# The last four sequences' stages of a four-layer stack get issue times of their own

## The chip, the cores and the metric

The kernel runs on one core of one Trainium2 chip. The metric is the device time of one execution in microseconds (us), the median of several runs. The core has engines with a queue each: PE (matrix multiply, with its weight loads), DVE (vector), ACT (scalar functions), POOL (general) and SP, which here only issues transfers. Each serves its queue in the order in which the program puts it.

## The reference

Sixteen sequences of 512 tokens with 256 features pass through four layers, each with a normalization before it and a residual sum behind it:

```
x = x + mamba(layernorm(x))        # a state scan over the 512 tokens, 16 states
x = x + fp4_ffn(layernorm(x))      # gate, up, down; 704 hidden
x = x + linear_attention(layernorm(x))   # 16 heads, causal
x = x + fp4_ffn(layernorm(x))      # the same weights again
```

An `fp4_linear` rounds its input in blocks of 16 to the nearest of eight magnitudes times a block scale, and multiplies with weights rounded likewise. The sequences are independent of each other. Within a sequence the four layers follow each other.

## The kernel before

**Stages.** All matrix products are in float32. For each sequence `b` there are four stages, written as Python generators that yield a number, their own estimate of the work just recorded:

- `scan(b)` (L850): `mamba` of `b` woven with `prologue` of `b + 1` (norm, projections, and the step sizes `dt` written to DRAM as `dd`). `mamba` takes 16 steps. In each, `spread` loads a decay tile `bar` by DMA from `dd` (four buffers, issued three steps ahead), ACT takes two exponentials and a square of it (L527, L530), DVE runs the scan (L548) and a multiply (L552) into `h`, and PE sums over the states into `py` (L558). After each half, `py` is copied to `yT` (L565), transposed (`pt_y`, L568) and added to `x` (L571).
- `ffn(0, "f", b)`: layer norm on DVE (L392 to L405, the power on POOL, L394), the rounding `fp4` (L230 to L252: `amax`, `half`, `inv`, `v`, `big`, with ACT's `big` at L248 in the middle), transposes `pt_f` (L418), then four chunks of 128 tokens. For each chunk `hidden` makes `pg` and `pu` (L605), the gated product `h` (L611 to L613) and its rounding, and `down` transposes it (`pt_h`, L627), copies it on ACT (`hqT`, L631 and L636), multiplies (`po`, L640) and adds to `x` (L377).
- `attention(b)`: `rstd` of the statistics, `pt_a` (L426, which waits for `diag_a`, made on ACT at L424 from `rstd`), `pqk` (L678), the feature maps (L684 to L686), the running key sums `run` and `pden` (L816 to L823), and then per chunk `pv`, `psc` (L722), the masked scores `sm` (L729), `pn` (L753), its copy `num` on ACT (L760), `pr` (L768), `yT` (L773), the state update `pkv` and `kv`, and the projection `pro` (L800) with its sum into `x` (L377).
- `last_ffn(b)`: the same FFN code under the letter `g`; its sum into `x` is L647, and then `x` goes out by DMA.

A tile's name carries the stage's letter; in this text its sequence is told in words ("`po_g` of 14, chunk 3").

**The order.** `run_all` (L865) decides in which order the stages' instructions are recorded. Each stage has a begin, a length and a total (`SCAN`, `FFN`, `ATTN`); it keeps a clock that starts at its begin and moves on by the yielded number times length over total, and the stage with the earliest clock records its next piece. The unit is one sequence: scan `b` begins at `b`, its first FFN at `b + 1`, its attention at `b + 2.1` and its last FFN at `b + 3.1`. So in the steady part four sequences are under way, each in another stage. After recording, the framework's scheduler places the instructions in each engine's queue, by readiness and by the recorded order as priority; the recorded order therefore shifts the queues but is not copied into them.

Behind sequence 15 there is no further scan, so the kernel drains: its first FFN is recorded beside attention 14 and the last FFN of 13, its attention beside the last FFN of 14, and its last FFN alone.

Of the kernel before, what the change touches and what calls it, by code (L numbers as in the profile page):

```python
# [32 lines left out]
def kernel(  # L33
# [19 lines left out]
    B, S, D = x.shape  # L53
# [37 lines left out]
    def load(b):  # L91
        xt = xp.tile([P, NC, D], F32, tag="x", name=f"x_{b}")
        nc.sync.dma_start(xt, x[b].rearrange("(c p) d -> p c d", p=P))
        return xt

    xs = [load(0)]
# [766 lines left out]
    SCAN, FFN, ATTN = 65.7, 40.2, 25.7  # L863

    def run_all(stages):  # L865


        under_way = []
        while stages or under_way:
            if not under_way or (stages and stages[0][0] <= min(u[0] for u in under_way)):  # L870
                begin, length, total, stage, *args = stages.pop(0)
                under_way.append([begin, length / total, stage(*args)])
                continue
            now = min(under_way, key=lambda u: u[0])
            try:
                now[0] += next(now[2]) * now[1]
            except StopIteration:
                under_way.remove(now)
# [12 lines left out]

    stages = []
    for b in range(B):
        if b > 0:
            stages.append((b, 1.0, SCAN, scan, b))
        stages.append((b + 1.0, 1.0, FFN, ffn, 0, "f", b, xs))
        stages.append((b + 2.1, 0.9, ATTN, attention, b, xs))
        stages.append((b + 3.1, 0.6, FFN, last_ffn, b))
    run_all(sorted(stages, key=lambda stage: stage[0]))


# [27 lines left out]
```

## Time and profile before

| | |
|---|---|
| Median of 3 runs | 2825.38 us (2824.58 to 2828.75) |
| The profiled execution | 2823.49 us, its span 2821.8 us |
| Mean granted clock of PE | 0.942 |
| PE busy | 2449.7 us, 87% of the span |
| DVE busy | 2430.5 us, 86% |
| ACT busy | 1492.1 us, 53% |
| The chain that ended last | DVE 40%, PE 36%, DMA 9%, ACT 9%, issue 3% |
| Loads of `bar` | 256 of 511 KB, 4.7 us each from issue to landing |

All times inside the execution are counted from the span's start. A float32 product shows as two PE records, a transpose as one. The busy time of an engine is the union of its records; PE's records are pipelined, so a busy PE is not PE at its peak. The granted clock is the share of full speed that PE's clock was given in a stretch. In a line of a timeline the columns are start, duration, engine, source line, operation, tiles written and read, shape, count, and in brackets the idle time before it with what ended it. In a line of the waits they are who waited for whom, the total in us, how often, and the longest.

### The profile page before, as it was taken

To read this page: it belongs to the slowest core of one execution; us is meant where nothing else is said; L and a number is where in the kernel's file an instruction comes from. 1 tells how busy PE (TensorE), PEld (TensorE's weight loads), DVE (VectorE), ACT (ScalarE), POOL (GpSimd) and SP (SyncE) were. 2 spreads that over 40 slices of the span, in tenths; PEclk is the share of its full clock that TensorE was granted. 3 is DMA by queue.
4 is the path that set the end of the run, shared out by engine and by line. 5 is a ranking of instruction groups with operands and counts; after the bars stand their busy time and mean duration, and the time that the engine had idled before them with its cause. 6 is when DMAs were issued, how large, how long until landed. Compare 5 with 4: busy or idle time off the path is not lost.

```text
span 2821.8 us, 34272 instructions
## 1 busy us (share of the span) xinstructions
PE 2449.7 (87%) x12907; PEld 1441.9 (51%) x12907; DVE 2430.5 (86%) x3689; ACT 1492.1 (53%) x2846; POOL 172.2 (6%) x171
## 2 busy tenths in 40 slices
PE   5677989799898989989898998989899898889886
PEld 3234545455555555555555555555555554556564
DVE  7898888898999898899989889998988999868465
ACT  4776564465646455464645556464555646333321
POOL 2000000000000010000001000000100000000000
PEclk7788999899999999999999999999999999999897
DMA  5533212222223131322313132131213213000000
GB/s 142 131 93 82 64 49 53 67 53 83 52 60 76 38 75 45 82 53 54 82 38 75 45 82 53 47 89 38 75 45 83 53 45 82 24 8 1 8 8 8
DMA packets 97146, 165.01 MB, mean 58 GB/s; under 512 B 8434, under 2 KB 92372, under 8 KB 96980
## 3 DMA queue, kind: packets, MB, share of 16 engines
q1 hardware_dynamic: 95360, 161.77, 22.3%
q8 instruction: 101, 1.65, 0.3%
q10 hardware_dynamic: 1620, 1.06, 0.1%
q14 instruction: 65, 0.53, 0.1%
HBM read 146.02 MB, written 16.78 MB: 58 GB/s over the span
## 4 chain that ended last, share of the span: by engine, by line
DVE 40%; PE 36%; DMA 9%; ACT 9%; issue 3%; POOL 2%; SPq 0%; POOLq 0%; ACTq 0%; DVEq 0%
DVE h L548 15%; DMA bar<-dd 9%; PE pg_g L605 5%; DVE h L552 4%; PE pu_g L605 4%; PE po_g L640 4%; PE pg_f L605 3%; PE pu_f L605 3%; PE py L558 3%; ACT bar L527 2%; PE pz L457 2%; DVE v_f L244 2%; DVE sm L729 2%; PE pqk L678 2%; ACT bar L530 1%
## 5 line engine op out<-in xcount | busy, mean ns | idle before, releaser
L548 DVE TENSOR_TENSOR_SCAN h<-bar,inp 128x1024 f32<-128x1024 f32 x256 | 579.4, 2277 | 13.9 <-PE py L558 7.6
L527 ACT ACTIVATE bar<-bar,a_col 128x511 f32<-128x511 f32 x512 | 352.4, 715 | 339.6 <-DMA bar<-dd 291.5
L558 PE MATMUL py<-h,red 128*32 128x512 f32 x1024 | 288.7, 645 | 119.3 <-DVE h L552 118.2
L552 DVE TENSOR_TENSOR h<-h,cm 128x1024 f32<-128x1024 f32 x256 | 311.1, 1218 | 0.6
L530 ACT ACTIVATE bar<-bar 128x1022 f32<-128x1022 f32 x256 | 269.3, 1052 | 3.0
L640 PE MATMUL po_g<-wdT,hqT_g 128*128 128x256 f32 (+1 forms) x768 | 214.3, 425 | 41.8 <-ACT hqT_g L631 41.8
L640 PEld LDWEIGHTS po_g<-wdT,hqT_g 128*128 128x128 f32 (+1 forms) x768 | 149.0, 206 | 120.3 <-ACT hqT_g L631 65.1
L640 PE MATMUL po_f<-wdT,hqT_f 128*128 128x256 f32 (+1 forms) x768 | 198.2, 400 | 9.6 <-ACT hqT_f L631 9.6
L605 PE MATMUL pg_g<-wgT,tT_g 128*128 128x352 f32 x512 | 190.7, 492 | 0.3 <-DVE sm L729 0.3
L640 PEld LDWEIGHTS po_f<-wdT,hqT_f 128*128 128x128 f32 (+1 forms) x768 | 137.5, 192 | 94.6 <-ACT hqT_f L636 29.0
L605 PE MATMUL pu_g<-wuT,tT_g 128*128 128x352 f32 x512 | 182.3, 480 | 0.0
L605 PE MATMUL pg_f<-wgT,tT_f 128*128 128x352 f32 x512 | 181.8, 478 | 0.0
L605 PE MATMUL pu_f<-wuT,tT_f 128*128 128x352 f32 x512 | 172.7, 460 | 3.4 <-DVE sm L729 3.0
L729 DVE TENSOR_TENSOR sm<-psc,causal 128x512 f32<-128x512 f32 x256 | 163.9, 681 | 10.8 <-PE psc L722 5.9
L611 ACT ACTIVATE h_g<-pg_g 128x352 f32<-128x352 f32 x128 | 59.1, 462 | 195.3 <-PE pg_g L605 195.1
L558 PEld LDWEIGHTS py<-h,red 128*32 128x32 f32 x1024 | 37.8, 110 | 221.6 <-DVE h L552 171.4
L605 PEld LDWEIGHTS pu_g<-wuT,tT_g 128*128 128x128 f32 x512 | 103.3, 202 | 60.7 <-issue 11.4
L763 POOL COPY dx<-den 128x256 f32<-128x256 f32 x64 | 42.2, 660 | 1482.7 <-PE pr L768 795.5
L248 ACT ACTIVATE big_f<-v_f 128x704 bf16<-128x704 f32 (+1 forms) x80 | 67.2, 840 | 122.3 <-DVE v_f L244 122.3
L605 PEld LDWEIGHTS pg_f<-wgT,tT_f 128*128 128x128 f32 x512 | 96.3, 196 | 66.9 <-issue 23.2
L612 DVE SCALAR_TENSOR_TENSOR h_g<-h_g,pg_g 128x352 f32<-128x352 f32 x128 | 65.5, 512 | 74.2 <-ACT h_g L611 72.8
L678 PE MATMUL pqk<-tT_a,w_qkv_sb 128*128 128x512 f32 x256 | 121.6, 614 | 7.4 <-ACT tT_a L430 7.4
(237 smaller groups left out, 4707.0 us busy)
## 6 DMA issues: line engine op xcount, KB each, us to landing
bar<-dd SPq DMA_DIRECT2D x256, 511.0 KB, 4.7
x<-in_L_attn_a_x_dram SPq DMA_DIRECT2D x16, 512.0 KB, 4.5
dd<-dt SPq DMA_DIRECT2D x128, 64.0 KB, 1.7
out_dram<-x SPq DMA_DIRECT2D x16, 512.0 KB, 4.4
w_qkv_sb<-in_L_attn_b_W_attn_dram ACTq DMA_DIRECT2D x1, 768.0 KB, 7.1
raw_d<-in_L_ffn_w_down_dram SPq DMA_DIRECT2D x1, 704.0 KB
raw_g<-in_L_ffn_w_gate_dram SPq DMA_DIRECT2D x1, 640.0 KB, 7.1
raw_u<-in_L_ffn_w_up_dram SPq DMA_DIRECT2D x1, 640.0 KB, 6.5
```

The source lines that it names most:

```text
L248: nc.scalar.activation(big, v, AF.Abs, scale=STEP)
L527: nc.scalar.activation(bar[:, i, 1:S], bar[:, i, 1:S], AF.Exp, scale=a_col[:, g : g + 1])
L530: nc.scalar.activation(bar[:, :, 1:S], bar[:, :, 1:S], AF.Square)
L548: nc.vector.tensor_tensor_scan(h.rearrange("p i t -> p (i t)"), bar.rearrange("p i t -> p (i t)"), inp.rearrange("p i t -> p (i t)"), 0.0, ...
L552: nc.vector.tensor_tensor(h, h, cm.unsqueeze(1).to_broadcast([P, 2, S]), ALU.mult)
L558: nc.tensor.matmul(py[32 * q : 32 * q + 32, :], red[:, j, :], (h0, h)[q // 2][:, q % 2, :], start=False, stop=(j == 3),)
L605: nc.tensor.matmul(pw[:, :HF], xqT[:, k, ts(c, P)], wT[:, k, cols], start=(k == 0), stop=(k == ND - 1),)
L611: nc.scalar.activation(hc, pg[:, :HF], AF.Tanh, scale=0.5)
L612: nc.vector.scalar_tensor_tensor(hc, hc, 1.0, pg[:, :HF], ALU.add, ALU.mult)
L640: nc.tensor.matmul(po[:, :D], hqT[:rows, r, :], wdT[:rows, r, :], start=(r == 0), stop=(r == NR - 1),)
L678: nc.tensor.matmul(pz, w_qkv_sb[:, k, ts(je, P)], xnT[:, k, :], start=(k == 0), stop=(k == ND - 1),)
L729: nc.vector.tensor_tensor(t, psc[g].rearrange("p (s t) -> p s t", t=P), causal.unsqueeze(1).to_broadcast([P, NH // 4, P]), ALU.mult,)
```

## The change

It gives the last four sequences begins and lengths of their own in `run_all`'s unit. The table is indexed by how far the sequence is from the last one; each entry names a stage (0 scan, 1 first FFN, 2 attention, 3 last FFN), its begin after 15, and its length. The other stages keep the old times, and no stage's code is touched.

```
     stages = []
     for b in range(B):
+        times = [(b, 1.0), (b + 1.0, 1.0), (b + 2.1, 0.9), (b + 3.1, 0.6)]
+
+        for stage, *time in {0: ((0, 0.0, 0.75), (1, 0.78, 0.7), (2, 1.5, 0.5), (3, 2.02, 0.4)), 1: ((1, 0.0, 0.75), (2, 0.8, 0.65), (3, 1.5, 0.5)), 2: ((2, 0.1, 0.7), (3, 0.9, 0.6)), 3: ((3, 0.1, 0.75),)}.get(B - 1 - b, ()):
+            times[stage] = (B - 1 + time[0], time[1])
         if b > 0:
-            stages.append((b, 1.0, SCAN, scan, b))
-        stages.append((b + 1.0, 1.0, FFN, ffn, 0, "f", b, xs))
-        stages.append((b + 2.1, 0.9, ATTN, attention, b, xs))
-        stages.append((b + 3.1, 0.6, FFN, last_ffn, b))
+            stages.append((*times[0], SCAN, scan, b))
+        stages.append((*times[1], FFN, ffn, 0, "f", b, xs))
+        stages.append((*times[2], ATTN, attention, b, xs))
+        stages.append((*times[3], FFN, last_ffn, b))
     run_all(sorted(stages, key=lambda stage: stage[0]))
```

In begin and end (begin plus length):

| Sequence | Stage | Before | After |
|---|---|---|---|
| 12 | last FFN | 15.1 to 15.7 | 15.1 to 15.85 |
| 13 | attention | 15.1 to 16.0 | 15.1 to 15.8 |
| 13 | last FFN | 16.1 to 16.7 | 15.9 to 16.5 |
| 14 | first FFN | 15.0 to 16.0 | 15.0 to 15.75 |
| 14 | attention | 16.1 to 17.0 | 15.8 to 16.45 |
| 14 | last FFN | 17.1 to 17.7 | 16.5 to 17.0 |
| 15 | scan | 15.0 to 16.0 | 15.0 to 15.75 |
| 15 | first FFN | 16.0 to 17.0 | 15.78 to 16.48 |
| 15 | attention | 17.1 to 18.0 | 16.5 to 17.0 |
| 15 | last FFN | 18.1 to 18.7 | 17.02 to 17.42 |

## The prediction

> **What bounds the kernel now.** I read the page's slices first, then the busy time by stretch of the closing part, then the waits there, then PE's timeline around the longest of them. The two programs as built differ only from 2382.1 us on (PE's first moved instruction; DVE's is at 2390.4, ACT's at 2369.5), so 2382 of the 2821.8 us are the same in both, and I price the rest.
>
> ```profile
> PE   5677989799898989989898998989899898889886
> DVE  7898888898999898899989889998988999868465
> PEclk7788999899999999999999999999999999999897
> ```
>
> One slice is 70.5 us. DVE runs at nine tenths until the last scan ends and then falls to 8, 6, 8, 4, 6, 5; PE stays at 8 or 9 up to the last slice. The drain is bound by PE and by the chain of the last sequence, not by DVE.
>
> ```profile
> core 0: us, PE busy (x) PEld busy (x) DVE busy (x) ACT busy (x) POOL busy (x), PEclk, DMA share, GB/s
> 2382.00:2543.00 161.00, 139.79 (x745) 85.37 (x744) 129.57 (x209) 63.92 (x135) 5.93 (x7) 0.93 0.09 23
> 2543.00:2661.00 118.00, 105.44 (x651) 71.54 (x649) 79.52 (x149) 34.67 (x89) 5.02 (x6) 0.97 0.02 5
> 2661.00:2766.00 105.00, 84.57 (x538) 56.38 (x538) 62.16 (x104) 28.51 (x65) 2.61 (x5) 0.86 0.02 6
> 2766.00:2821.80 55.80, 42.91 (x144) 28.41 (x144) 29.32 (x49) 11.45 (x26) 0.00 (x0) 0.84 0.03 10
> ```
>
> These are four stages, cut where PE starts sequence 15's first FFN (2543), its attention (2661) and its second FFN (2766). I call them A, B, C, D. PE is idle 21, 13, 20 and 13 us in them, 67 in all. Its work is the same in both kernels, so 67 us less what cannot be filled is all that reordering can win, apart from the clock.
>
> ```profile
> DVE x L377 <- PE po_f L640: 15.6, 5, 3.9
> PE pt_g L418 <- DVE xn_g L252: 12.3, 2, 12.1
> PE pt_h_g L627 <- DVE h_g L252: 10.5, 3, 3.9
> PE pt_a L426 <- ACT diag_a L424: 8.9, 2, 5.1
> ACT bar L527 <- DMA bar<-dd: 7.9, 7, 3.0
> ```
>
> Totals, counts, and the longest, from 2382 on. PE's long waits are handovers: to attention (`pt_a`), to the last FFN (`pt_g`), and one for a quantized hidden chunk (`pt_h_g`).
>
> ```profile
> 2653.01 3.05 PE L640 MATMUL po_f<-wdT,hqT_f 128*128 128x256 f32 x12 [0.46 <-ACT hqT_f L631]
> 2661.13 4.23 PE L426 MATMUL pt_a<-diag_a,x 128*128 128x128 f32 x16 [5.06 <-ACT diag_a L424]
> 2694.12 1.54 PE L627 MATMUL pt_h_g<-ident,h_g 128*128 128x128 f32 x6 [3.94 <-DVE h_g L252]
> 2695.91 5.29 PE L640 MATMUL po_g<-wdT,hqT_g 128*128 128x256 f32 x12 [0.25 <-ACT hqT_g L631]
> 2766.32 1.97 PE L418 MATMUL pt_g<-ident,xn_g 128*128 128x128 f32 x8 [12.12 <-DVE xn_g L252]
> ```
>
> Each wait is paid twice: the same 12 `po` records take 3.05 us when PE comes from work and 5.29 after the 3.94 us wait. The granted clock is 0.50 over 2659.6 to 2669.8 and 2755.2 to 2772.2, and 0.51 over 2693.7 to 2700.6.
>
> **The measure.** Every instruction is priced at the mean busy time that its line and shape add to its engine in the trace (the sum is the page's 2449.7 for PE), and these are added up in each program's order. "PE 2195" means 2195 us of PE work ahead of an instruction.
>
> - Scan 15's last multiply ends: DVE 2235.2 before (at 2487.8 us), 2222.7 after.
> - Scan 15's last transposes (`pt_y`): PE 2195.2 (at 2500.4), after 2173.9.
> - `pt_a` of 14: PE 2218.2 (2531.5), after 2210.3.
> - `pt_f` of 15, the start of B: PE 2228.3 (2543.1), after 2230.1.
> - `po_f` of 15, chunk 3: PE 2330.8 (2653.0), after 2322.9.
> - `pt_a` of 15, the start of C: 2334.0 (2661.1) in both.
> - `po_g` of 14, chunks 0 and 3: PE 2360.5 and 2391.9, after 2368.7 and 2409.3.
> - `pt_g` of 15, the start of D: 2412.5 (2766.3) in both.
>
> Nothing is added or removed: instructions, DMAs and ACT's 33 table loads are equal in number, and SP's order is the same, so no transfer is issued past another. The cost of the edit is only in who waits.
>
> **Stage A.** The scan passes 12.5 us of DVE work and 21.3 us of PE work. Before, DVE did 89.4 us of work up to the last multiply in 97.4 us (2390.4 to 2487.8); after, it has 76.9, at that rate 83.8, so the multiply ends at 2474.2. PE reaches its last `py` after 77.0 us of work instead of 91.7; at its old rate (91.7 in 108.8 us) that is 91.4 us, at 2473.5. The two meet, as before, so I add no wait. The last `py`, the copy `yT` and `pt_y` end near 2477.7. From there 55.5 us of PE work stand ahead of B. PE did the corresponding 32.4 us at 77% before, wait for `pt_a` included; B runs at 90%. I take 88%, nearer to B, because 21 us of ready work now lie there: 63.1 us, so B starts at 2540.8, against 2543.1: **2.3 us gained**, and 1.8 us of B's work already done. Bounds by the two rows: 2550 at 77%, 2536 at 95%. Inside it the wait at `pt_a` of 14 changes place: on ACT the copy `num` of 13's last chunk now stands behind `diag_a` of 14, so `pro` of 13 waits for `rstd_a`; on DVE the quantization of 12's last chunk now stands ahead of `var_a`. I keep about 3 us of the old 3.86 for it.
>
> **Stage B.** PE's work is 103.9 instead of 105.7: **1.8 us**. The 5.06 us wait at `pt_a` of 15 came because `po_f` chunk 3 was the last work ahead of it. After, 7.9 us of FFN 13 (`po_g` chunks 2 and 3) stand between. The chain from the end of `pro` of 14 to `pt_a` took 9.4 us (2651.7 to 2661.1); two more steps of `v_g` (1.22 each) come ahead of `var_a` on DVE while two small ones move forward, so about 11; PE has 15.9 us of work in that time. But `hqT_g` of 13's chunk 3 is queued on ACT behind `diag_a`, which leaves 12.7 us certain, still more than 11. I charge 1 us: **4.1 us gained**. Bounds: none gained (FFN 13's fill starves), 5.06. FFN 15's chunk chain has 30 us or more of PE work between `pg_f` and its `pt_h`, so it adds no wait.
>
> **Stage C.** Three terms. (1) With the 5.06 us wait goes its slow clock: `pt_a` took 4.23 us; the same 16 took 3.85 after the 3.86 us wait, and the 16 `pqk` records 9.22 against 7.68 there: 1.9 at least, 2.7 if `pt_a` falls to about 3.1 (16 by the gain of `po`). I take **2.7**. (2) The 3.94 us wait for `h_g` of 14: DVE's work ahead minus PE's was 6.3 us there and is now -3.7, so it goes, and with it 5.29 - 3.05 and 1.54 - 0.82 (the next chunk's): **6.9**. (3) `po_g` of 14's chunk 3 with its transposes (4.0 us) now stands behind attention's last `pro`, inside the 12.12 us wait of `pt_g`: **3.9**. Against them, `pro` of 15's chunk 0 moves up 18.1 us and that difference becomes +4.2; zero wait lay at 6.3 - 3.9 = 2.4, so it may wait **1.8**. DVE's `x` of L647 now stands inside the last norm, 0.35 us, hidden if `po_g` ends within the 6 us before it. C falls by 11.7. Bounds: 0 if the waits only change place, 16 if even the 1.8 is hidden and `po_g` chunk 1 (4.61 us) also runs in 3.05.
>
> **Stage D** holds the same 37 us of work with nothing beside it: 0, within 2 either way by its first `pg`.
>
> **Sum.** 2.3 + 1.8 + 4.1 + 11.7 = 19.9, say 19.5. The profiled execution took 2823.5 us (span 2821.8), 1.9 below the median of 2825.4; from the median: **2806**.
>
> A rule of the Trainium skill bears on the second payment. "TensorE: Matmul & The Clock Gate", Part 1, says that PE's clock halves after an idle window of about 3.4 us, that the window runs free of the kernel, and that one shouldn't fit to a cold count. The trace agrees that waits of 3.9 us and more are followed by 0.50. By it the two waits that go and the one that stays are each worth up to 1.7 us (half of 3.4) more or less by chance, and the time would be an estimated 2801 to 2811.
>
> **Rivals.**
> 1. *Slower: the last scan doesn't close up.* If its steps are limited by the load of `bar` and ACT's two exponentials and square instead of by what else is queued on DVE, `pt_y` stays near 2500.4 with 21.3 us more PE work behind it. At A's old rate of 84% the 55.5 us then take 66.1, B starts at 2567.2, 24.1 late, less 1.8 of work done, 4.1 in B and 11.7 in C: 6.5 slower, 2832. The sign turns once `pt_y` comes after 2494, 16 us later than forecast. For: ACT waited 7 times for `bar`, up to 3.0. Against: four buffers, the tightest reuse is 24 us of DVE work apart, and a load (4.7) with ACT's 2.5 needs 7.2. 0.13.
> 2. *No change: the waits change place.* `pro` of 13 in A (6.6 us more DVE lead than before, plus slow clock), `hqT_g` behind `diag_a` in B, `yT` behind FFN 14's quantization in C, each 4 to 7 us: 16 to 20 together, 2822 to 2826. For: PE's work is conserved, and each queue is served in order. 0.12.
> 3. *Larger gain: PE keeps 95% in A and C also hides its 1.8:* 5 + 1.8 + 4 us more than forecast, 2794. 0.17.
> 4. *Forecast,* 2799 to 2817: 0.58.
>
> A measurement can tell about 0.2%, 5.6 us. Faster takes the forecast and rival 3: 0.75; rival 2 is mostly the same, 0.12; slower is 0.13. The range runs from rival 3 with 2 us below it, 2792, to the upper edge of rival 2, 2826.
>
> **What would show it.** In the profile after: the last `h` L552 near 2474, `pt_f` of 15 near 2541, `pt_a` near 2653 with an idle below 2 us ahead of it, no wait over 2 us at `pt_h_g` of 14, `pt_g` still 12 us after attention's last `pro` but with `po_g` inside, and D unchanged near 55.5. It is wrong if `pt_f` of 15 comes after 2550, or if `pt_g` of 15 follows `pt_a` by more than 100 us.

## The result, and the profile after

The changed kernel took **2804.11 us** (median of 4 runs, 2796.54 to 2810.31); the kernel before took 2826.86 beside it (4 runs). The ratio is 0.9919, 95% interval 0.9893 to 0.9945. The forecast was 2806. The profiled execution was the longest of the four: 2810.31 us, span 2808.6, mean granted clock 0.944.

The page's slices, as before 1/40 of the span each (70.2 us):

```profile
PE   5677889799888898989889898989989898899996
DVE  7898888898899889989989989898899988987665
PEclk7788999999999999999999999999999999999998
```

DVE's last five slices are 8, 7, 6, 6, 5 instead of 6, 8, 4, 6, 5: the dip in the last stages has been filled, and PE is at nine tenths in the four slices ahead of the last.

The windows of the four stages, cut at the same instructions as before: A from the same place in the program, B at `pt_f` of 15, C at `pt_a` of 15, D at `pt_g` of 15.

```profile
core 0: us, PE busy (x) PEld busy (x) DVE busy (x) ACT busy (x) POOL busy (x), PEclk, DMA share, GB/s
2395.00:2549.00 154.00, 135.50 (x762) 82.74 (x761) 131.12 (x211) 64.75 (x139) 5.33 (x7) 0.97 0.09 25
2549.00:2658.70 109.70, 101.74 (x637) 69.16 (x637) 83.99 (x150) 34.78 (x87) 4.60 (x6) 0.98 0.00 1
2658.70:2753.30 94.60, 79.79 (x539) 52.77 (x539) 58.33 (x102) 27.36 (x62) 2.61 (x5) 0.94 0.04 12
2753.30:2808.60 55.30, 42.74 (x144) 28.43 (x144) 29.05 (x48) 11.45 (x26) 0.00 (x0) 0.84 0.03 10
```

Before they lasted 161, 118, 105 and 55.8. A is 7 shorter, B 8, C 10, D the same. But A begins at 2395, where 2382 was expected: this execution came 12.7 us later to the first scan step of sequence 15 than the profiled one before (2344.0 against 2331.3), although both programs are the same up to beyond that step. So the sharper clock is the one that starts there, and every stage below is counted from it. By it the drain took 490.5 us before and **464.6** after, 25.9 less.

The waits from 2395 to the end (who waited for whom, total, times, longest):

```profile
ACT bar L527 <- DMA bar<-dd: 16.4, 6, 4.2
PE pt_g L418 <- DVE xn_g L252: 8.6, 1, 8.6
PE pt_h_g L627 <- DVE h_g L252: 6.6, 2, 3.8
PE py L558 <- DVE h L552: 5.8, 3, 3.8
PE pt_y L568 <- ACT yT L565: 4.3, 1, 4.3
DVE x L377 <- PE po_f L640: 2.9, 4, 1.5
```

`pt_a` waited 8.9 us in all and has no row any more. `pt_g` fell from 12.3 to 8.6. `pt_h_g` lost one of its three waits, the 3.94 us one (10.5 to 6.6). `py` and `pt_y` wait a little more (3.2 and 3.0 before), and ACT waits twice as long for the loads of `bar` (7.9 before), as a scan would that is given more room and runs nearer to its own chain.

PE's timeline at the places that were shown of before:

```profile
2647.06 3.05 PE L640 MATMUL po_f<-wdT,hqT_f 128*128 128x256 f32 x12 [0.46 <-ACT hqT_f L631]
2651.37 3.05 PE L640 MATMUL po_g<-wdT,hqT_g 128*128 128x256 f32 x12 [0.46 <-ACT hqT_g L631]
2655.68 3.05 PE L640 MATMUL po_g<-wdT,hqT_g 128*128 128x256 f32 x12 [0.46 <-ACT hqT_g L631]
2658.66 2.42 PE L426 MATMUL pt_a<-diag_a,x 128*128 128x128 f32 x16
2692.64 1.13 PE L800 MATMUL pro<-w_o_sb,yT 128*128 128x256 f32 x4 [1.98 <-DVE yT L773]
2699.37 3.83 PE L640 MATMUL po_g<-wdT,hqT_g 128*128 128x256 f32 x12 [0.25 <-ACT hqT_g L631]
2753.30 1.94 PE L418 MATMUL pt_g<-ident,xn_g 128*128 128x128 f32 x8 [8.64 <-DVE xn_g L252]
```

Two chunks of FFN 13 (`po_g`) now stand between `po_f` and `pt_a`, and `pt_a` has no idle time ahead of it and runs in 2.42 us instead of 4.23. The 3.94 us wait at `pt_h_g` of 14 is gone, but `pro` of 15's first chunk waits 1.98. The last wait is 8.64 instead of 12.12.

### The profile page after: what moved, and what is told of

It reads as the page before. It is cut to its first block, busy times and chain, and to the rows that moved or that the text cites. A ratio compares the mean times of both kernels' runs of the same rounds, so it can differ in the third digit from the quotient of the medians.

```text
span 2808.6 us, 34278 instructions
## 1 busy us (share of the span) xinstructions
PE 2443.9 (87%) x12907; PEld 1436.5 (51%) x12907; DVE 2432.7 (87%) x3689; ACT 1491.0 (53%) x2846; POOL 171.8 (6%) x171
## 4 chain that ended last, share of the span: by engine, by line
DVE 40%; PE 35%; DMA 10%; ACT 9%; issue 4%; POOL 2%; SPq 0%; POOLq 0%; ACTq 0%; DVEq 0%
DVE h L548 15%; DMA bar<-dd 10%; PE pg_g L605 5%; DVE h L552 4%; PE pu_g L605 4%; PE po_g L640 3%; PE pg_f L605 3%; PE pu_f L605 3%; PE py L558 3%; ACT bar L527 2%; DVE sm L729 2%; PE pz L457 2%; DVE v_f L244 1%; ACT bar L530 1%; PE po_f L640 1%
## 5 line engine op out<-in xcount | busy, mean ns | idle before, releaser
L640 PE MATMUL po_g<-wdT,hqT_g 128*128 128x256 f32 (+1 forms) x768 | 205.9, 412 | 40.2 <-ACT hqT_g L631 40.2
L605 PEld LDWEIGHTS pu_f<-wuT,tT_f 128*128 128x128 f32 x512 | 97.1, 190 | 58.9 <-DVE sm L729 5.2
```

Of the source, the lines that this page charges most:

```text
L605: nc.tensor.matmul(pw[:, :HF], xqT[:, k, ts(c, P)], wT[:, k, cols], start=(k == 0), stop=(k == ND - 1),)
L640: nc.tensor.matmul(po[:, :D], hqT[:rows, r, :], wdT[:rows, r, :], start=(r == 0), stop=(r == NR - 1),)
```

## The experiments

All but e1 and e9 edit the table in the change's `for` line; its keys are as above (0 is sequence 15). "From scan 15" is the time from its first scan step to the end of the span. The stage lengths of every profile:

| Kernel | last multiply | `pt_y` | A | B | C | D | from scan 15 |
|---|---|---|---|---|---|---|---|
| before | 156.6 | 169.1 | 211.8 | 118.0 | 105.2 | 55.5 | 490.5 |
| after | 138.6 | 145.0 | 204.8 | 109.8 | 94.6 | 55.3 | 464.6 |
| e1 after again | 138.8 | 145.3 | 207.6 | 109.8 | 94.7 | 55.6 | 467.6 |
| e2 FFN 14 stretched | 157.0 | 169.5 | 213.6 | 119.9 | 100.7 | 53.5 | 487.7 |
| e3 FFN 13 and 14 stretched | 156.0 | 167.8 | 212.2 | 111.3 | 94.7 | 55.6 | 473.8 |
| e4 scan 15 only | 137.3 | 139.9 | 215.6 | 115.2 | 105.0 | 55.4 | 491.2 |
| e5 FFN 14 early | 139.1 | 145.5 | 206.2 | 110.8 | 101.7 | 55.5 | 474.2 |
| e6 FFN 13 early | 138.8 | 145.2 | 205.9 | 113.1 | 101.4 | 53.7 | 474.1 |
| e7 give way alone | 165.7 | 186.0 | 242.1 | 122.8 | 63.3 | 54.7 | 482.9 |
| e8 FFN 14 later | 138.9 | 145.4 | 206.1 | 110.8 | 104.1 | 53.5 | 474.4 |
| e9 filler products | 137.4 | 143.8 | 204.5 | 110.9 | 97.3 | 53.5 | 466.2 |
| e10 FFN 14 to 17.02 | 137.7 | 144.2 | 206.5 | 109.8 | 92.2 | 54.9 | 463.4 |
| e11 FFN 14 earlier, longer | 137.9 | 144.4 | 206.7 | 109.8 | 93.9 | 53.4 | 463.8 |

The first two columns are counted from the same step: the end of the last multiply, and the start of the last `pt_y`. Each row is one profiled execution. The eight profiles with the changed kernel's order in A (after, e1, e5, e6, e8 to e11) spread over 204.5 to 207.6 there, which tells how finely one may read.

### e1: the changed kernel once more

> The changed kernel once more. Handover theory (the gain is 8 us in stage A, 8 in B, 11 in C, as the first profile shows): 20 to 27 us faster than before, and D near 55.5. On the 13 us by which the first profile of the changed kernel was later than before already at the last scan's first step, though the instructions up to there are the same: if that is chance of one execution, this profile's first step of the last scan lies anywhere between 2325 and 2350; if the changed program is slower there for a cause of its own, it lies at 2340 to 2348 again.

No edit. Median 2808.2 of 6 (2799.64 to 2816.68) against 2825.19 of 23: 0.9934 (0.9911 to 0.9956). The profiled execution reached scan 15 at 2330.3, 13.7 earlier than the first one of the same kernel, and its span was 2797.9. Stages B, C and D repeat to 0.3 us and A to 2.8. So the late start of the first profile belongs to that execution and not to the order. The medians differ by 17.0 us, less than the 20 to 27 expected; from scan 15 the profile is 22.9 shorter than before.

### e4: only the last scan closes up

```
- for stage, *time in {0: ((0, 0.0, 0.75), (1, ...), ...), 1: ..., 2: ..., 3: ...}
+ for stage, *time in {0: ((0, 0.0, 0.75),)}
```

> Only scan 15 is changed, to the length 0.75; all other stages keep the old times. The last scan passes 33 us of PE work, and from the transposes of FFN 15 on the order is that of before. Handover theory: PE is the bound of the drain and its work is only put behind the scan, so the start of FFN 15 moves by less than 4 us and the time by -4 to +3. Scan theory: 15 to 22 us faster. Rival of the prediction (the last scan does not close up): the last multiply stays within 3 us of before and the time is 5 us or more above before.

Median 2828.38, ratio 1.0006 (0.9991 to 1.0021). Stages A to C of e4, cut as above:

```profile
2389.00:2554.00 165.00, 140.73 (x748) 84.97 (x747) 131.04 (x210) 64.24 (x136) 6.03 (x7) 0.91 0.09 23
2554.00:2669.00 115.00, 102.10 (x651) 69.53 (x649) 79.56 (x149) 34.50 (x88) 5.01 (x6) 0.99 0.02 5
2669.00:2774.00 105.00, 84.37 (x539) 56.33 (x539) 62.44 (x104) 28.35 (x64) 2.60 (x5) 0.86 0.02 6
```

PE's waits in stage A of e4:

```profile
PE py L558 <- DVE h L552: 10.9, 4, 7.4
PE pt_a L426 <- ACT diag_a L424: 3.4, 1, 3.4
```

The scan did close up: its last multiply ends 19.3 us earlier and `pt_y` 29.2 earlier. Yet A ends 3.8 us later. PE met the scan earlier, waited 7.4 us for one `h`, and had the other sequences' work still ahead of B. C is 105.0 with the 5.07 us wait at `pt_a` of 15 still there. An early scan alone is worth nothing, because the end of A is PE's work and not DVE's: behind the last `pt_y` PE was busy for 67.8 of the 74.5 us up to B.

### e2 and e3: only the last FFNs are spread out

```
- {0: ..., 1: ..., 2: ..., 3: ...}
+ e2: {1: ((3, 2.1, 0.9),)}
+ e3: {1: ((3, 2.1, 0.9),), 2: ((3, 1.1, 0.95),)}
```

> Only the last FFN of 14 is changed: begin 17.1 as before, length 0.9 in place of 0.6, so that it ends with attention 15. The order of PE and DVE from attention 15 on is that of the changed kernel, up to there that of the kernel before. Handover theory: C falls from 105 to 95 to 97, nothing else moves, 8 to 11 us faster than before. Scan theory (the gain comes from the last scan closing up): 0 to 3 us faster.

> As the one before, and the last FFN of 13 begins at 16.1 as before and has the length 0.95 in place of 0.6, so that two of its chunks stand between FFN 15's last product and attention 15. Scan 15 is as before. Handover theory: B falls from 118 to 110 to 112 and C to 93 to 97, 15 to 19 us faster than before. Scan theory: 0 to 5 us faster.

e2: 2818.38, ratio 0.9971 (0.9959 to 0.9983). e3: 2811.03, 0.9946 (0.9927 to 0.9966). These two kernels leave the last scan, FFN 15 and the attentions at their old times. e2 spreads FFN 14 alone: C falls by 4.5, while B keeps its 5.1 us wait at `pt_a`. I had expected C at 95 to 97 and 8 to 11 us; it came to 100.7 and 6.8, and only 2.8 from scan 15. e3 also stretches FFN 13 over the handover: B falls by 6.7 and C by 10.5, both near the full change (8.2 and 10.5), and from scan 15 it is 16.7 shorter of the 22.9 to 25.9 that the full change gives. What e3 lacks lies in A (212.2 against about 206). Its B and C lie within what I expected, its medians (14.2 us faster) just below the 15 to 19.

What e2's C lacks is in part clock. PE's windows around the 1.98 us wait for `yT`, which both kernels have, of e1:

```profile
2680.20:2683.60 3.40, 1.96 (x7) 0.99 0.00 0
2683.60:2690.40 6.80, 6.55 (x18) 0.50 0.00 0
```

and of e2:

```profile
2698.70:2702.10 3.40, 2.01 (x26) 0.99 0.02 5
2702.10:2715.80 13.70, 12.15 (x28) 0.50 0.00 0
```

The columns are span, PE busy with its records, granted clock, DMA. The same wait is followed by 6.8 us at half clock in one and by 13.7 in the other. Half of the difference, up to 3.4 us, is what e2's C pays beyond the rest. The handover doesn't decide this: e9 below has it filled and also shows 13.7.

### e5 and e6: one of the two spreads undone

```
- 1: (..., (3, 1.5, 0.5))      - 2: (..., (3, 0.9, 0.6))
+ e5: 1: (..., (3, 1.5, 0.33))  + e6: 2: (..., (3, 0.9, 0.42))
```

> The changed kernel, but the last FFN of 14 has the length 0.33 in place of 0.5, so that attention 15 and this FFN stand in the order of before; stages A and B are those of the changed kernel. From the first step of the last scan to the end before took 490.5 us, the changed kernel 464.6 and 467.6. Handover theory: A and B keep their 12 to 15 us, C is 98 to 102 (the 3.9 us wait at the transposes of 14's chunk 0 and the 12.1 us wait of the last FFN are back, the slow clock behind the attention's start is not): 470 to 476. If the gain hangs on the drain as a whole (any piece undone spoils the rest): 480 or more.

> The changed kernel, but the last FFN of 13 has the length 0.42 in place of 0.6, so that nothing of it stands between FFN 15's last product and attention 15; the rest is the changed kernel's order. Handover theory: the 5.06 us wait at the start of attention 15 is back and with it 10 us at half clock, B is 114 to 118 and C 97 to 101, and from the last scan's first step to the end it takes 474 to 482. If the handover is hidden anyway: 463 to 469.

e5: 2810.28, ratio 0.9919 (0.9902 to 0.9936); from scan 15 474.2, within the expected 470 to 476. e6: 2815.71, 0.994 (0.9925 to 0.9954); 474.1, at the near edge of 474 to 482, with B 0.9 below and C 0.4 above what I expected. By the medians neither can be told from the changed kernel (0.9919, and 0.9934 in e1); what each part is worth is read from the stages of the profiles. The longest waits of e5 in C:

```profile
PE pt_g L418 <- DVE xn_g L252: 12.1, 1, 12.1
PE pt_h_g L627 <- DVE h_g L252: 3.9, 1, 3.9
```

and of e6 from the handover to its C's end:

```profile
PE pt_g L418 <- DVE xn_g L252: 8.6, 1, 8.6
PE pt_a L426 <- ACT diag_a L424: 4.3, 1, 4.3
PE pro L800 <- DVE yT L773: 3.2, 5, 2.0
```

Each undone part brings back its wait: FFN 14's spread is what shortens `pt_g` and removes the `h_g` wait (7.0 us of C), FFN 13's is what covers `pt_a` (3.3 of B). e6's C is 6.7 longer too, with its FFN 14 untouched: there again the 1.98 us wait is followed by 13.7 us at half clock.

### e7: those ahead give way, the last sequence keeps its old times

```
- {0: ((0, 0.0, 0.75), ...), 1: ..., 2: ..., 3: ...}
+ {1: ..., 2: ..., 3: ...}
```

> Only the stages of 12, 13 and 14 have the new times; those of sequence 15 keep the old ones. The last FFN of 14 is then through 3 us of PE work before attention 15 starts, which runs alone with 41 us of PE work. Handover theory: the handover to attention 15 is filled, but the attention has nothing to fill its own chain, 10 us or more of new waits of PE in it: 3 to 20 us slower than before. If giving way alone brings the gain: 10 us or more faster.

2822.27, ratio 0.9963 (0.9949 to 0.9978); 482.9 from scan 15, 7.6 less than before. This misses what I had written, 3 to 20 us slower. The work of 13 and 14 goes ahead of sequence 15 and lengthens A by 30.3 and B by 4.8, but C then is attention 15 alone, and it took only 63.3. PE's longest waits in it and at its end:

```profile
PE pt_g L418 <- DVE xn_g L252: 12.1, 1, 12.1
PE psc L722 <- ACT ko L715: 2.0, 1, 2.0
PE pden L823 <- DVE run L819: 1.4, 1, 1.4
```

Attention keeps PE dense by itself; only the norm behind it leaves PE empty. The filler is needed behind attention, not inside it.

### e8, e10, e11: where FFN 14 ends

```
- 1: (..., (3, 1.5, 0.5))
+ e8:  (3, 1.5, 0.6)    e10: (3, 1.5, 0.52)    e11: (3, 1.45, 0.55)
```

> The changed kernel, but the last FFN of 14 has the length 0.6 in place of 0.5. Attention 15's last projection then stands 6.5 us of PE work earlier, and 12.1 us of FFN 14 behind it in place of 5.6 with the projection. Handover theory: the 8.65 us wait before the last FFN falls below 4 us, D loses 1 to 3 us of half clock, and from the last scan's first step to the end it takes 455 to 461 (changed: 464.6 and 467.6), 25 to 32 us faster than before. Rival (the last FFN's chain sets the end and the filler stands in its way on DVE or ACT): 463 or more.

> The changed kernel, but the last FFN of 14 has the length 0.52 in place of 0.5. The start of attention 15 keeps its order; its last projection stands 4.0 us of PE work earlier, with both last products of FFN 14 behind it. Filler theory: the 8.65 us wait before the last FFN falls to 4 to 6, the last projection waits 1 to 2 us more for its yT, C falls from 94.7 to 91 to 93.5. Rival (as when that length was 0.6: the filler's own chain on DVE and ACT delays the last norm): C 95 or more.

> The changed kernel, but the last FFN of 14 begins at 16.45 in place of 16.5 and has the length 0.55 in place of 0.5. Attention 15's first projection then stands 6.5 us of PE work later, the rest of the end as in the changed kernel. Lead theory (a projection waits once DVE's work ahead of it exceeds PE's by more than 2.4 us; it was 4.2 there and is 0.6 now): the 1.98 us wait at this projection goes, with it the slow stretch of 6.8 us behind it, and C falls from 94.7 to 89 to 92.5. Rival (another wait of the same length takes its place): C 94 to 96.

e8: 2816.68, ratio 0.9937 (0.992 to 0.9953); from scan 15 474.4, where 455 to 461 were expected. Its PE waits in C:

```profile
PE pt_h_g L627 <- DVE h_g L252: 4.9, 1, 4.9
PE pro L800 <- DVE yT L773: 2.6, 1, 2.6
PE pden L823 <- DVE run L819: 2.1, 1, 2.1
PE psc L722 <- ACT ko L715: 2.0, 1, 2.0
PE pt_g L418 <- DVE xn_g L252: 1.6, 1, 1.6
```

The `pt_g` wait is nearly gone, and C is 9.4 longer than in e1. On DVE the rounding of FFN 14's last chunk now stands among the steps of the last norm: from the last `pro` to `pt_g` it takes 19.5 us instead of 13.0. The filler delays what it should only cover, and attention's start, left alone, shows e7's waits.

e10: 2802.66 (5 runs), ratio 0.9915 (0.9897 to 0.9933); C 92.2, in the expected 91 to 93.5. Its two longest:

```profile
PE pt_g L418 <- DVE xn_g L252: 4.2, 1, 4.2
PE pro L800 <- DVE yT L773: 3.0, 3, 2.0
```

It fills 4.4 us more of the last gap without getting into the norm, and has the shortest drain of all, 463.4. In the medians it can't be told from the changed kernel (0.9915 and 0.9919, with intervals of 0.002 and 0.003 either way), so it is not shown to be better.

e11: 2806.47, ratio 0.9924 (0.9906 to 0.9942); C 93.9, short of the expected 89 to 92.5. Its two longest waits in C:

```profile
PE pt_g L418 <- DVE xn_g L252: 8.6, 1, 8.6
PE pkv L784 <- ACT kt L779: 3.6, 1, 3.6
```

The wait for `yT` went, and one of 3.6 us for `kt` came in its place.

### e9: filler products in the last gap

```
  (in ffn, behind the norm; the product's bank is read by no one)
+ if i == 1 and b == B - 1:
+     warm = bank("warm")
+     for _ in range(7):
+         nc.tensor.matmul(warm, xt[:, NC - 1, 0:P], xt[:, NC - 2 : NC, :].rearrange(...), start=True, stop=True)
```

> The changed kernel, with seven extra products of 128x512 of PE (about 6.4 us, written to a bank that nobody reads) between FFN 14's last product and the transposes of the last FFN, inside the 8.65 us wait; they depend on attention's last sum into x. Nothing is taken away. Slow-clock theory (a wait is paid twice: as idle time and as slow records behind it): the wait falls below 3 us, the first pg and pu of the last FFN take 1.2 in place of 2.5 and 2.0 us, and D falls from 55.5 to 51 to 53.5, C unchanged within 1: 461 to 465 from the last scan's first step to the end. Rival (the last FFN is bound by its chain through ACT and DVE, so PE's speed is hidden): D 55 to 56.

2804.82, ratio 0.9927 (0.9908 to 0.9946); from scan 15 466.2, just above the expected 461 to 465. PE's timeline at the gap (line numbers behind the insertion are 7 higher):

```profile
2736.89 6.28 PE L590 MATMUL warm<-x 128*128 128x512 f32 x14
2745.62 1.77 PE L418 MATMUL pt_g<-ident,xn_g 128*128 128x128 f32 x8 [2.45 <-DVE xn_g L252]
2747.21 2.43 PE L612 MATMUL pg_g<-wgT,tT_g 128*128 128x352 f32 x4
```

The idle time fell to 2.45 us, and D was 53.5, within the expected 51 to 53.5. But the first `pg` still took 2.43 us and not 1.2, and C was 97.3, 2.6 longer than in e1, where I had expected it within 1: its wait for `yT` was followed by 13.7 us at half clock. And D was 53.4 to 53.7 in e2, e6, e8 and e11 too, which have no filler. In e1 the clock came back about 6 us after `pt_g` began, in e2 and e6 3.5 and 3.9 after, behind nearly equal waits (8.65, 8.7, 8.6). So the experiment doesn't show that the filler is worth anything: 2 us of D go with where the slow stretch falls.

## Why the prediction was right, and where it was not

The total held: 19.5 us forecast, 22.7 by the medians, 17.0 in e1's. From scan 15, 19.9 stood in the sum, and 25.9 and 22.9 were measured.

**Where the work lies.** Right: all of it comes out of idle PE time and clock in A, B and C; D is unchanged. What the prediction undercounted is the clock. From scan 15's first step on PE was idle for 73.2 us before, 60.3 after and 61.3 in e1, and its 2336 records, the same work, were busy for 417.3, 404.3 and 406.3. So only half of the gain is filled idle time (12.9 and 11.9 us); the other half is records that ran faster (13.0 and 11.0), the mean granted clock having risen from 0.91 to 0.95 and 0.94. The prediction priced the clock in C alone, at 5.7 us (2.7, and 6.9 less the 3.94 of waiting). That the total came out is in part luck: A and B were 3.4 and 2.3 short, C 1.2 long.

**Stage A: right in sign, 2.3 forecast, 5.7 measured** (about 206.1 against 211.8, mean of after, e1, e5, e6, e8). The mis-sized term is the 88% for PE after `pt_y`. `pt_y` came 24 earlier (23 forecast), and the 55.5 us of PE work behind it then took 59.2 us in after and 61.7 in e1, where 63.1 were forecast, which is 94 and 90%. In all of A, PE's idle time fell by 2.3 us (e1: 1.3) and its busy time by 4.6 (2.9), though 1.8 us more work was done in it: this gain is mostly clock. The wait of 3 us that I kept at `pro` or `pt_a` did not come; those at `py` and `pt_y` grew by 2.6 and 1.3, where I had added none. The multiply itself ended 18 earlier instead of 13.6. e4 adds what the prediction had only assumed: the early scan gains nothing unless the other stages' new times keep PE busy meanwhile (PE was idle for 31.0 us in A of e4, 25.0 and 26.0 in after and e1).

**Stage B: 5.9 forecast, 8.2 measured.** The handover is the right mechanism; e2 against e3, and e6, show it. The 1 us that I charged at `pt_a` was not paid: no idle stands ahead of it in after and e1. By the windows, PE's idle time in B fell from 12.6 to 8.0 and its busy time by 3.7, of which 1.8 were forecast as moved work.

**Stage C: 11.7 forecast, 10.5 measured, out of errors that cancel.** Term 1, the slow clock of the handover: `pt_a` 4.23 to 2.42 and `pqk` 9.22 to 7.13, which is 3.9, where 2.7 was forecast. (Scaled like `po`, 5.29 to 3.05, `pt_a` falls to 2.44, not to the 3.1 that the prediction has.) Term 2 is the step that failed: the 3.94 us wait went, but a stretch at half clock stayed. It stands now behind the 1.98 us wait for `yT`, here with the same length. PE's windows there, of before and of after:

```profile
2693.70:2700.60 6.90, 6.23 (x17) 0.51 0.00 0
2694.20:2701.00 6.80, 6.55 (x17) 0.50 0.00 0
```

So 6.9 less 1.8 became 3.94 less 1.98, or 2.0. I charged the new wait its length alone and no slow records behind it. Term 3: 3.5 filled in the last gap, forecast 3.9. And `po_g` of 14's chunk 1, left in the prediction as a bound, lost most of its wait (1.71 to 0.46) and ran in 3.05 instead of 4.61, 2.8. The lines of these records, two of before and two of after:

```profile
2665.61 9.22 PE L678 MATMUL pqk<-tT_a,w_qkv_sb 128*128 128x512 f32 x16 [0.25 <-ACT tT_a L430]
2711.02 4.61 PE L640 MATMUL po_g<-wdT,hqT_g 128*128 128x256 f32 x12 [1.71 <-ACT hqT_g L631]
2661.54 7.13 PE L678 MATMUL pqk<-tT_a,w_qkv_sb 128*128 128x512 f32 x16 [0.45 <-ACT tT_a L430]
2718.59 3.05 PE L640 MATMUL po_g<-wdT,hqT_g 128*128 128x256 f32 x12 [0.46 <-ACT hqT_g L631]
```

Together 12.2, which is 1.7 above the measured 10.5; 1.1 of it are shorter waits that grew (by the windows idle time in C fell by 5.6, by the waits named here by 6.7).

By the rule of "TensorE: Matmul & The Clock Gate", Part 1 of the Trainium skill, an idle window of about 3.4 us precedes the half clock; if idle means without any work, 1.98 us don't fill one. The runs differ: with PE busy 1.56 of the 3.4 us just before, half clock followed, so the measurement decides. That the window runs free of the kernel agrees: in each of the 13 profiles all changes of the clock lie on one grid of 3.41 us, and the same wait gave slow stretches of 6.8 and 13.7 us.

**The rivals.** Rival 1, the scan that doesn't close up, did not happen, though ACT waited 16.4 us for `bar` instead of 7.9. Rival 2, waits that change place, is true of single waits (e11, and 1.98 for 3.94) and false of the sum. Rival 3's larger gain came about in A (94% in one profile, for its 95%) and not in C; its 10.8 us would have given 2795, not 2794.

**What stays open.** The 1.98 us wait was followed by 6.8 us at half clock in three profiles (after, e1, e3), by 13.7 in three (e2, e6, e9) and by 10.2 in e10. It goes with where the slow stretch begins: 0.9 to 1.3 us ahead of the wait's end in those with 13.7, 1.5 to 2.0 behind it in those with 6.8, 2.2 behind it in e10. Why this sets the length wasn't isolated, and which of the table's entries earn the gain in A was not tested one by one.

## What to carry to other kernels

In a drain, look for the work that is bound to nothing and lay it behind the chains that leave the bottleneck empty, the handover's norm above all: e3, with two table entries, won 16.7 of 23 to 26 us, while closing up the last scan alone won nothing. The filler has to end before the chain that it covers reaches its engine's queue; e8 stretched it by 0.1 of the unit and, by the profiles, lost 7 to 10 us again. Price a wait by what the clock does behind it as well as by its length, and where a stage's cost is a few us, count from an instruction that both programs share.

## What the runs showed of the hardware that I had not expected

- Instructions that are the same in every kernel took different times: the first step of scan 15 lay between 2330.3 and 2344.0 us in 13 profiles, 13.7 us or 0.6% apart; the two ends of that range are profiles of one and the same kernel (e1, after), and e1 and e3, on one chip, are 11.2 apart. Up to that step PE was busy for 2029.4 us in e1 and 2039.7 in after with equally many records, at a mean clock of 0.95 and 0.94, and DVE for 2085.8 and 2085.3: most of the difference is where half clock fell. It isn't all: e8 came to the step at 2341.8 with PE busy for 2032.8.
- PE's clock went to half after waits much shorter than the shortest I had counted (3.86): 1.98 us sufficed, with PE busy for 1.6 to 2.2 of the 3.4 us before. It goes with how much of one stretch of that grid PE works. In the 13 profiles, from 300 us on, PE by its records was busy for less than 40% of a 3.41 us stretch at full clock 326 times, and half clock followed every time; for 65% or more 7854 times, and it followed 7 times; in between the outcome varied.
- The slow stretches in the drain lasted 3.4, 6.8, 10.2, 13.7 or 17.1 us, multiples of about 3.4, but for those that the end cuts off.
